# Edge sums of attention step 0: bitwise AND of the u8 blocks and a ones-column matmul instead of block products and a masked diagonal

## The chip, the cores and the metric

The kernel runs on one core of a Trainium2 chip. A core has five engines that run their own instruction queues: TensorE (PE in the profile, with its weight loads as PEld), VectorE (DVE), ScalarE (ACT), GpSimd (POOL) and SyncE (SP, which only issues DMAs here). The metric is the device time of the whole program in microseconds; lower is better.

## The reference, cut to what matters

A graph network of four layers on N = 4096 nodes with D = 256 features and a 0/1 adjacency matrix. Each layer's result is added to x and normalised.

```python
# layer 1: two steps of attention (A keeps the top of each row's softmax)
R = S + I;  R = R / R.sum(-1)              # S is the adjacency matrix here
for n in range(2):
    A  = top_p_attention(Xa, W1, W2, W3)
    Xf = R @ Xf
    Xa = A @ Xa
    Z  = Z + Xf @ U1[n].T + Xa @ U2[n].T
...
# layer 2
neighbor_node_features = adj @ node_features
neighbor_edge_features = einsum('ij,ji->i', adj, edge_features)   # edge_features is adj
support = concat(node_features, neighbor_node_features, neighbor_edge_features)
return support @ weight + bias
```

The change concerns the einsum: the edge sum of node i is the number of j with adj[i,j] and adj[j,i] both 1. It doesn't depend on features, and layer 2 reads it from the tile `nef` (128 partitions x 32 row tiles).

## The kernel before

Rows come in 32 tiles of 128. Columns come in 8 chunks of 512, called g0 to g7 here; a chunk has GP = 4 blocks of 128x128. Layer 0 runs to about 378 us, step 0 of layer 1 from there to about 1340 us, then step 1, then layers 2 and 3.

Step 0 is one software pipeline over the row tiles (`run_step`, with `pieces` for one tile's turn). In one turn TensorE goes through the chunks; in each chunk it computes logits for the tile two ahead (L381), adds gathered rows of x weighted by attention for the tile whose top entries are known (L730, weights from VectorE's dg, L728), and does the R product of the tile whose turn it is (`neighbours`). Between these, pieces for other tiles are hung into chosen chunks (`ops`): the exponentials (ScalarE L419), the choice of the top 16 entries (VectorE MAX8 L400, and two FIND_INDEX8 at L497 over rows of 4096), the flag of rows that need more entries (TensorE L559 and L560, VectorE L562 to L567) whose numbers GpSimd scatters into a list in DRAM (`list_d`, L573, 128 rows of 4 bytes), the 16 gathers of 128 rows of 1 KB (GpSimd L639, eight buffers: gather k+8 is emitted behind product k), and afterwards the mixing with U (TensorE L791, VectorE h at L793) and the keys of the new rows (TensorE L799). The first four row tiles of step 0 have only their R product, while the pipeline fills.

`neighbours(n, i, g, acc_r, pn, xf)` does one chunk of the R product for row tile i. Every second chunk SP loads a u8 tile adj8 (L648, three buffers). ScalarE casts 512 columns to float32r (`a`, L650), and four matmuls of 128x512 add into acc_r (L653), with xf held as a high and a low half of 256 columns each. L655 adds the identity's share at the end.

In step 0 it also computes the edge sums. Every fourth chunk GpSimd loads 256 KB of the transposed blocks as u8 (adjn8, L659, two buffers); ScalarE casts 512 columns (`b`, L662); four matmuls of 128x128 multiply blocks of `a` by blocks of `b` and add into the bank pn (`nef_ps`, L665). The edge sums are the diagonal of the sum.

`r_end` ends the tile: ScalarE scales one half of acc_r into xf_new (L674), VectorE adds the other (L675), VectorE multiplies pn by the identity and sums its rows into a column of nef (L679), SP stores xf_new (L681). acc_r and nef_ps each have one PSUM bank in step 0, so the next tile's first product waits until L675 has read acc_r. The same functions serve step 1, without pn.

Step 1 begins by loading the keys from DRAM (k_d), transposing them into kS (L1059), and loading xa (L1066).

Every engine takes its own queue in order, but that order isn't the order of the text: instructions of different pieces are interleaved on each engine when the program is built.

Of the kernel before, what the change touches and what calls it, by code (L numbers as in the profile page):

```python
# [11 lines left out]
F32 = mybir.dt.float32  # L12
I32 = mybir.dt.int32
U8 = mybir.dt.uint8
F32R = mybir.dt.float32r
AF = mybir.ActivationFunctionType
ALU = mybir.AluOpType
AX = mybir.AxisListType
# [3 lines left out]
P = 128  # L22
# [26 lines left out]
def gnn_stack(ctx, tc, x, adjt, adjn, w0, b0, w1, w2t, w3t, u1t, u2t, ln_g, ln_b, w2, b2, w3, b3, out):  # L49
# [3 lines left out]
    nc = tc.nc  # L53
    N = x.shape[0]
    NT = N // P
    LC = min(512, N)
    NLC = N // LC
# [9 lines left out]
    dram = ctx.enter_context(tc.tile_pool(name="dram", bufs=1, space=DRAM))  # L67
    ps_two = ctx.enter_context(tc.tile_pool(name="ps_two", bufs=1, space=PSUM))
    ps_acc = ctx.enter_context(tc.tile_pool(name="ps_acc", bufs=1, space=PSUM))
    ps_tr = ctx.enter_context(tc.tile_pool(name="ps_tr", bufs=2, space=PSUM))  # L70
# [7 lines left out]
    def half(bank):  # L78
        turns[bank] ^= 1
        return (mm_bank if bank == "mm" else acc_bank)[:, turns[bank], :]  # L80
# [10 lines left out]
    ident = const.tile([P, P], F32, name="ident")  # L91
    make_identity(nc, ident)
    ones_col = const.tile([P, 1], F32, name="ones_col")
# [5 lines left out]
    nef = const.tile([P, NT], F32, name="nef")  # L99
# [12 lines left out]
    list_d = [dram.tile([N + P, 1], I32, name=f"list{n}_d") for n in range(STEPS)]  # L112

    adj8_d = [dram.tile([P, NT, P], U8, name=f"adj8_{it}_d") for it in range(NT)]
    h_d = dram.tile([N + P, D], F32, name="h_d")
    k_d = dram.tile([N + P, P], F32, name="k_d")

# [5 lines left out]
    def rows(t, it):  # L123
        return t[it * P : (it + 1) * P, :]

    def all_rows(t):
        return t.rearrange("(t p) d -> p t d", p=P)
# [86 lines left out]
    with tc.tile_pool(name="l0", bufs=1) as l0, tc.tile_pool(name="l0w", bufs=2) as l0w:  # L214
# [9 lines left out]
        for c in range(2):  # L224
            ps = half("mm")
# [10 lines left out]
        def l0_main(it):  # L236
            acc = ps_acc.tile([P, 512], F32, tag=("acc", "nef")[it % 2], name="acc")

            W = J0 * P
            sums = l0w.tile([P, W], F32, tag="sums", name="sums")  # L240

            now = {}

            def piece(it, c):

                if c % 2 == 0:
                    now["a8"] = a8 = l0w.tile([P, 2 * JP, P], U8, tag="a8", name="a8", bufs=5)
                    s = slice(c * JP, (c + 2) * JP)
                    nc.gpsimd.dma_start(a8, adjt[it, :, s, :])
                    nc.sync.dma_start(adj8_d[it][:, s, :], a8)  # L250
                a = l0w.tile([P, JP, P], F32R, tag="adjt", name="a", bufs=4)
                nc.scalar.copy(a, now["a8"][:, c % 2 * JP : (c % 2 + 1) * JP, :])  # L252
                return a

            def partial(c, a):
                a = a.bitcast(F32).rearrange("p j i -> p (j i)")
                for k in range(0, JP * P, W):
                    if c == 0 and k == W:
                        nc.vector.tensor_add(sums, a[:, :W], a[:, W : 2 * W])
                    elif c > 0:  # L260
                        nc.vector.tensor_add(sums, sums, a[:, k : k + W])
                if c + 1 == NJP:
                    for k in (W // 2, W // 4):
                        nc.vector.tensor_add(sums[:, :k], sums[:, :k], sums[:, k : 2 * k])

            adj_matmul(l0w, acc, it, lambda jt: x0h[:, jt, :], piece, partial)
            return acc, sums
# [40 lines left out]
        for it in range(NT + 1):  # L308
            if it >= 1:
                agg = l0_agg(acc, l0_degrees(it - 1, sums))  # L310
            if it < NT:
                acc, sums = l0_main(it)
# [9 lines left out]
    with tc.tile_pool(name="l1", bufs=1, reuse_waits="tile") as l1:  # L322

        cur = {"late": False, "n": 0, "nef_done": False}
# [9 lines left out]
                                channel_multiplier=-1)  # L334
        ident_r = l1.tile([P, P], F32R, name="ident_r")
        nc.vector.tensor_copy(ident_r, ident)
        upto = l1.tile([P, PAD], F32, name="upto")
        nc.gpsimd.iota(upto, pattern=[[1, PAD]], base=0, channel_multiplier=0, allow_small_or_imprecise_dtypes=True)

# [9 lines left out]
        def load_u(n):  # L349
            for name, src in (("u1", u1t), ("u2", u2t)):  # L350
                t = l1.tile([P, 2, D], F32, tag=name, name=name)
                nc.scalar.dma_start(t, src[n].rearrange("(c p) o -> p c o", p=P))
                cur[name] = t
# [49 lines left out]
        QW = N // NQ  # L403

        spare_row = l1.tile([P, 4 * QW], U8, name="spare_row")
# [236 lines left out]
        GP = LC // P  # L642

        def neighbours(n, i, g, acc_r, pn, xf):

            if g % 2 == 0:
                cur["a8"] = cur["w"].tile([P, 2 * GP, P], U8, tag="adj8", name="adj8", bufs=3)
                nc.sync.dma_start(cur["a8"], adj8_d[i][:, g * GP : (g + 2) * GP, :])  # L648
            a = cur["w"].tile([P, GP, P], F32R, tag="adjq", name="adjq", bufs=2)
            nc.scalar.copy(a, cur["a8"][:, g % 2 * GP : (g % 2 + 1) * GP, :])  # L650
            for j in range(GP):
                jt = g * GP + j
                nc.tensor.matmul(acc_r, a[:, j, :], xf[:, jt, :], start=(jt == 0), stop=False)  # L653
            if g + 1 == NLC:
                nc.tensor.matmul(acc_r, ident_r, xf[:, i, :], start=False, stop=True)  # L655
            if pn is not None:
                if g % (NLC // 2) == 0:
                    cur["b8"] = cur["w"].tile([P, NT // 2, P], U8, tag="adjn8", name="adjn8", bufs=2)
                    nc.gpsimd.dma_start(cur["b8"], adjn[i, :, g * GP : g * GP + NT // 2, :])  # L659
                b = cur["w"].tile([P, GP, P], F32R, tag="adjn", name="adjn", bufs=2)  # L660
                k = g % (NLC // 2) * GP
                nc.scalar.copy(b, cur["b8"][:, k : k + GP, :])  # L662
                for j in range(GP):
                    jt = g * GP + j
                    nc.tensor.matmul(pn[:, :P], a[:, j, :], b[:, j, :], start=(jt == 0),  # L665
                                     stop=(jt == NT - 1))

        def r_acc(i):

# [2 lines left out]
        def r_end(i, acc_r, pn):  # L672
            xf_new = work.tile([P, D], F32, tag="xf_new", name="xf_new", bufs=1)
            nc.scalar.activation(xf_new, acc_r[:, :D], AF.Copy, scale=rs[:, i : i + 1])  # L674
            nc.vector.scalar_tensor_tensor(xf_new, acc_r[:, D:], rs[:, i : i + 1], xf_new, op0=ALU.mult, op1=ALU.add)  # L675
            if pn is not None:

                junk = spare_row.bitcast(F32)[:, :P]
                nc.vector.scalar_tensor_tensor(junk, pn[:, :P], 1.0, ident, op0=ALU.mult, op1=ALU.mult,  # L679
                                               accum_out=nef[:, i : i + 1])  # L680
            nc.sync.dma_start(rows(xf_d, i), xf_new)  # L681

        def r_product(n, i, xf):
# [8 lines left out]
        def pieces(n, st, nxt, ops, rs_now=()):  # L692
# [60 lines left out]
            if with_r:  # L753
                r_end(i, acc_r, pn)
# [286 lines left out]
        for n in range(STEPS):  # L1041
            cur["n"] = n
            with tc.tile_pool(name=f"step{n}", bufs=2, reuse_waits="tile") as cur["w"], \
                    tc.tile_pool(name=f"late{n}", bufs=1, reuse_waits="tile") as cur["lw"]:
                es = [cur["w"].tile([P, N + PAD], F32, tag=f"e{k}", name="e", bufs=1) for k in range(2 + n)]
                if n == 0:
                    cur["xa"] = x1
                    cur["qs"] = [query(x1[:, i, :]) for i in range(2)]
                    cur["xf"] = load_halves(es[1], x1, None)
                else:  # L1050
                    cur["g"] = load_bcast(cur["lw"], ln_g, "g_sb")
                    cur["qs"] = first_queries(xa_d)
                    k_rows = es[1][:, :N].rearrange("p (t d) -> p t d", d=P)
                    for c in range(NLC):
                        s = slice(c * GP, (c + 1) * GP)
                        nc.sync.dma_start(k_rows[:, s, :], all_rows(k_d[:N, :])[:, s, :])
                        ps = ps_tr.tile([P, 4, P], F32, tag="tr", name="kt_ps")
                        for j in range(GP):
                            nc.tensor.transpose(ps[:, j, :], k_rows[:, c * GP + j, :], ident)  # L1059
                        k = kS[:, c * LC : (c + 1) * LC].rearrange("p (j d) -> p j d", d=P)  # L1060
                        (nc.vector.tensor_copy if c % 2 else nc.scalar.copy)(k, ps[:, :GP, :])
                    cur["xf"] = cur.pop("next")
                    cur["xa"] = xa = xpool.tile([P, NT, D], F32, tag="X", name="xa")
                    for c in range(NJP):
                        s = slice(c * JP, (c + 1) * JP)
                        nc.scalar.dma_start(xa[:, s, :], all_rows(xa_d[:N, :])[:, s, :])  # L1066
                load_u(n)
                run_step(n, es)

# [128 lines left out]
```

## Time and profile before

| what | us |
|---|---|
| median of 3 runs (lowest, highest) | 3308.88 (3306.8, 3313.18) |
| the profiled execution's time | 3340.46 |
| its span | 3338.8 |
| TensorE busy, whole span | 3024.1 |
| VectorE busy | 2395.2 |
| ScalarE busy | 1873.3 |
| L665, 1024 matmuls of 128x128 in step 0, busy | 150.0 |
| L679 in step 0, 32 instructions, busy | 9.0 |
| L662, 256 casts of 128x512, busy | 159.3 |
| L497, 64 searches in step 0, busy | 282.8 |

The profile is of one execution, which took 31.6 us longer than the median of the runs; sums of durations are to be held against its own span. The mean TensorE clock granted in it was 0.964 of full speed. Busy times of TensorE's matmuls overlap one another, since matmuls are pipelined and their ends are modelled; the distance between starts is what a matmul costs.

Costliest groups of step 0 on its edge sums, in the view that keeps shapes apart (columns: line, engine, operation, output and inputs, shapes, count, then busy us and mean ns of one, then the idle time before them and what ended it):

```profile
L662 ACT CAST adjn<-adjn 128x512 fp32r<-128x512 uint8 x256 | 159.3, 622 | 1.0 <-DMA adjn<-in_adjn 1.0
L665 PEld LDWEIGHTS nef_ps<-adjn,adjq 128*128 128x128 f32 x1024 | 157.3, 192 | 23.8 <-ACT adjn L662 0.6 <-issue 0.2
L665 PE MATMUL nef_ps<-adjn,adjq 128*128 128x128 f32 x1024 | 150.0, 266 | 0.0
L659 POOL DMA_DIRECT2D adjn<-in_adjn x64 | 37.6, 588 | 64.3 <-ACT adjn L662 50.0 <-ACT te L512 7.0 <-issue 6.9
```

### The profile page before, as it was taken

The page shows a single profiled execution, that of the slowest core. Times are in us where ns is not written, and L with a number is a line of the kernel's source. Part 1 is how long each engine was busy: PE and PEld are TensorE (multiplying, and loading weights), DVE is VectorE, ACT ScalarE, POOL GpSimd, SP SyncE. Part 2 cuts the span into 40 slices and gives each one's busy share as a digit, 9 for nine tenths or more (in the row PEclk, how much of TensorE's full clock was granted, in tenths as well). Part 3 has the DMA queues.
Part 4 walks back from the last instruction along what each step waited for, and adds up shares of the span by engine and source line. Part 5 has one row for each costly group of instructions (what it writes and reads, how often), then busy time and mean ns, then how long its engine had stood idle before and what let it go on. Part 6 is the DMA issues. An engine that isn't in the chain of part 4 may idle for free. (4 is left out here: it accounts for less than half of the span.)

```text
span 3338.8 us, 46384 instructions
## 1 busy us (share of the span) xinstructions
PE 3024.1 (91%) x14600; PEld 2462.3 (74%) x14600; DVE 2395.2 (72%) x7120; ACT 1873.3 (56%) x3162; POOL 781.6 (23%) x915
## 2 busy tenths in 40 slices
PE   6999888999999998779998898999999796999998
PEld 5888667777877777557887777877788554888886
DVE  7888858777777777346997888799799683444444
ACT  3555666766766665436555454555465333666664
POOL 1111245656666666100000001000100001000000
PEclk9999999999999998889999999999999898999999
DMA  9888366777777676331000211011111143333332
GB/s 174 139 142 138 71 103 119 134 125 135 135 133 123 122 134 144 94 116 42 25 23 21 32 29 37 28 31 37 29 34 34 32 142 117 114 109 106 100 110 81
DMA packets 247858, 300.17 MB, mean 90 GB/s; under 512 B 34672, under 2 KB 201520, under 8 KB 247600
## 3 DMA queue, kind: packets, MB, share of 16 engines
q0 software_dynamic: 46576, 104.94, 23.1%
q1 hardware_dynamic: 188800, 180.93, 18.7%
q10 hardware_dynamic: 12224, 11.23, 1.1%
q8 instruction: 118, 1.93, 0.3%
q14 instruction: 140, 1.15, 0.2%
HBM read 331.17 MB, written 66.45 MB: 119 GB/s over the span
## 5 line engine op out<-in xcount | busy, mean ns | idle before, releaser
L653 PE MATMUL acc_r<-xh,adjq 128*128 128x512 f32 x2048 | 616.2, 431 | 27.3 <-ACT adjq L650 20.4
L738 PE MATMUL acc_bank<-xa,at 128*128 128x256 f32 x2304 | 569.5, 388 | 29.5 <-ACT at L716 29.0
L639 POOL DMA_INDIRECT G<-x_d,cols x512 | 498.8, 974 | 334.1 <-PE acc_bank L730 155.8
L167 PE MATMUL acc<-xh,a 128*128 128x512 f32 x2048 | 516.5, 405 | 23.1 <-DMA a<-adj_d 15.6
L738 PEld LDWEIGHTS acc_bank<-xa,at 128*128 128x128 f32 x2304 | 424.9, 194 | 91.3 <-ACT at L716 39.9
L650 ACT CAST adjq<-adj 128x512 fp32r<-128x512 uint8 x512 | 315.8, 619 | 307.6 <-PE acc_r L653 95.5
L400 DVE MAX8 cand<-e 128x8 f32<-128x256 f32 x1024 | 381.8, 416 | 138.5 <-ACT e L382 115.2
L653 PEld LDWEIGHTS acc_r<-xh,adjq 128*128 128x128 f32 x2048 | 381.0, 192 | 126.9 <-ACT adjq L650 45.8
L167 PEld LDWEIGHTS acc<-xh,a 128*128 128x128 f32 x2048 | 384.8, 191 | 108.8 <-ACT xh L143 22.7
L382 ACT COPY e<-lg 128x512 f32<-128x512 f32 x552 | 320.2, 586 | 204.4 <-PE lg L381 173.4
L191 POOL TENSOR_TENSOR rstd<-ve,mhalf 128x1 f32<-128x1 f32 x168 | 103.3, 615 | 1377.5 <-DVE ve L189 1332.9
L381 PE MATMUL lg<-kS,q 128*128 128x512 f32 x1104 | 396.1, 444 | 21.0 <-ACT e L382 11.6
L1078 ACT CAST a<-a 128x1024 fp32r<-128x1024 uint8 x256 | 267.8, 1048 | 158.0 <-PE acc L167 121.3
L730 PE MATMUL acc_bank<-G,dg 128*128 128x256 f32 x1024 | 277.1, 392 | 32.8 <-DVE dg L728 13.8
L497 DVE FIND_INDEX8 cols<-top,e 128x8 uint32<-128x4096 f32 x64 | 282.8, 4419 | 0.0
L730 PEld LDWEIGHTS acc_bank<-G,dg 128*128 128x128 f32 x1024 | 194.0, 193 | 82.5 <-DMA G<-x_d,cols 20.3
L167 PE MATMUL acc<-yh,a 128*128 128x512 f32 x1024 | 233.7, 390 | 0.0
L716 ACT COPY at<-at_ps 128x512 f32<-128x512 f32 x296 | 173.8, 589 | 102.5 <-PE at_ps L713 100.8
L252 ACT CAST a<-a 128x1024 fp32r<-128x1024 uint8 x128 | 133.6, 1049 | 156.4 <-PE acc L167 121.4
L167 PEld LDWEIGHTS acc<-yh,a 128*128 128x128 f32 x1024 | 192.1, 188 | 39.7
L381 PEld LDWEIGHTS lg<-kS,q 128*128 128x128 f32 x1104 | 184.5, 194 | 45.2 <-ACT e L382 20.6
L713 PE MATMUL at_ps<-ident,e 128*128 128x128 f32 x1184 | 183.5, 279 | 14.7 <-DVE e L630 14.6
(281 smaller groups left out, 4634.2 us busy)
## 6 DMA issues: line engine op xcount, KB each, us to landing
adj<-adj_d SPq DMA_DIRECT2D x256, 128.0 KB
a<-adj_d SPq DMA_DIRECT2D x256, 128.0 KB
a<-in_adjt POOLq DMA_DIRECT2D x64, 256.0 KB
adj_d<-a SPq DMA_DIRECT2D x64, 256.0 KB
adjn<-in_adjn POOLq DMA_DIRECT2D x64, 256.0 KB
x_d<-x SPq DMA_DIRECT2D x64, 128.0 KB
G<-x_d,cols POOLq DMA_INDIRECT x512
xf_d<-xf_new SPq DMA_DIRECT2D x64, 128.0 KB
```

Of the source, the lines that this page charges most:

```text
L167: nc.tensor.matmul(acc, a[:, j, :], halves(jt), start=(jt == 0), stop=(jt == NT - 1))
L381: nc.tensor.matmul(pl[:, :LC], q[k], kS[:, s], start=(k == 0), stop=(k == 1))
L382: nc.scalar.copy(l[:, s], pl[:, :LC])
L400: nc.vector.max(dst[:, 8 * g : 8 * g + 8], src[:, g * GW : (g + 1) * GW])
L497: nc.vector.max_index(st["at"][:, 8 * r : 8 * r + 8], t8, st["e"][:, :N])
L639: nc.gpsimd.indirect_dma_start(out=g, out_offset=None, in_=x1_d, in_offset=bass.IndirectOffsetOnAxis(ap=st["at"][:, k : k + 1], axis=0))
L650: nc.scalar.copy(a, cur["a8"][:, g % 2 * GP : (g % 2 + 1) * GP, :])
L653: nc.tensor.matmul(acc_r, a[:, j, :], xf[:, jt, :], start=(jt == 0), stop=False)
L713: nc.tensor.transpose(ps[:, j, :], e[:, (g * G + j) * P : (g * G + j + 1) * P], ident)
L730: nc.tensor.matmul(acc_a, dg[:, k % 4, :], st["G"][k], start=(k == 0), stop=(k == KEPT - 1))
L738: nc.tensor.matmul(acc_a, ats[g][:, j, :], cur["xa"][:, jt, :], start=(jt == 0), stop=(jt == NT - 1))
L1078: nc.scalar.copy(a, a8)
```

## The change

Both inputs of the edge sum are 0 or 1, so the product of two elements is their AND, and the sum over j can be taken by a column of ones.

- Every second chunk of step 0 VectorE computes the bitwise AND of the adj8 tile and the matching half of adjn8, in place in adjn8, as 128x256 words of 32 bits (128 instructions). The load of adjn8 is emitted ahead of it, and so ahead of the chunk's casts.
- ScalarE's cast of `b` is the same instruction on the ANDed bytes.
- TensorE's four 128x128 products a chunk become one matmul: a column of 128 ones, times `b`'s 512 columns, added over the chunks into one row of 512 in pn. Each column of the row holds a quarter of a node's sum.
- At the tile's end ScalarE copies the row out of PSUM, into the spare row, and SP stores it to a row of `nef_d` in DRAM. VectorE's masked sum is gone.
- At the start of step 1 SP loads the 32 rows of 512; VectorE adds the four parts of each; TensorE transposes 32x128; VectorE copies the result to nef.

The lines after the change: adjn8 load L656, AND L659, acc_r's matmuls L664, cast of `b` L670, ones matmul L671, xf_new L680, row copy L684, store L685; searches L500, h L798, keys L804.

```diff
+    nef_d = dram.tile([NT, LC], F32, name="nef_d")
...
+        ones_r = l1.tile([P, 1], F32R, name="ones_r")
+        nc.vector.tensor_copy(ones_r, ones_col)
...
             if g % 2 == 0:
                 cur["a8"] = cur["w"].tile([P, 2 * GP, P], U8, tag="adj8", name="adj8", bufs=3)
                 nc.sync.dma_start(cur["a8"], adj8_d[i][:, g * GP : (g + 2) * GP, :])
+                if pn is not None:
+
+                    if g % (NLC // 2) == 0:
+                        cur["b8"] = cur["w"].tile([P, NT // 2, P], U8, tag="adjn8", name="adjn8", bufs=2)
+                        nc.gpsimd.dma_start(cur["b8"], adjn[i, :, g * GP : g * GP + NT // 2, :])
+                    k = g % (NLC // 2) * GP
+                    a32, b32 = (t.rearrange("p j i -> p (j i)").bitcast(I32) for t in (cur["a8"], cur["b8"][:, k : k + 2 * GP, :]))
+                    nc.vector.tensor_tensor(b32, b32, a32, op=ALU.bitwise_and)
             a = cur["w"].tile([P, GP, P], F32R, tag="adjq", name="adjq", bufs=2)
...
             if pn is not None:
-                if g % (NLC // 2) == 0:
-                    cur["b8"] = cur["w"].tile([P, NT // 2, P], U8, tag="adjn8", name="adjn8", bufs=2)
-                    nc.gpsimd.dma_start(cur["b8"], adjn[i, :, g * GP : g * GP + NT // 2, :])
                 b = cur["w"].tile([P, GP, P], F32R, tag="adjn", name="adjn", bufs=2)
                 k = g % (NLC // 2) * GP
                 nc.scalar.copy(b, cur["b8"][:, k : k + GP, :])
-                for j in range(GP):
-                    jt = g * GP + j
-                    nc.tensor.matmul(pn[:, :P], a[:, j, :], b[:, j, :], start=(jt == 0),
-                                     stop=(jt == NT - 1))
+                nc.tensor.matmul(pn[:1, :LC], ones_r, b.rearrange("p j i -> p (j i)"), start=(g == 0), stop=(g + 1 == NLC))
...
             if pn is not None:
 
-                junk = spare_row.bitcast(F32)[:, :P]
-                nc.vector.scalar_tensor_tensor(junk, pn[:, :P], 1.0, ident, op0=ALU.mult, op1=ALU.mult,
-                                               accum_out=nef[:, i : i + 1])
+                row = spare_row.bitcast(F32)[:1, QW - LC :]
+                nc.scalar.copy(row, pn[:1, :LC])
+                nc.sync.dma_start(nef_d[i : i + 1, :], row)
             nc.sync.dma_start(rows(xf_d, i), xf_new)
...
+                    parts = es[2][:NT, :LC]
+                    nc.sync.dma_start(parts, nef_d)
+                    sums = es[2][:NT, LC : LC + P]
+                    nc.vector.tensor_reduce(sums, parts.rearrange("t (j i) -> t i j", i=P), axis=AX.X, op=ALU.add)
+                    ps = ps_tr.tile([P, 4, P], F32, tag="tr", name="nef_ps")
+                    nc.tensor.transpose(ps[:, 0, :NT], sums, ident[:NT, :NT])
+                    nc.vector.tensor_copy(nef, ps[:, 0, :NT])
```

## The prediction

> **What bounds the kernel now.** I read the busy row first, then the groups of instructions, then the windows of step 0 (which runs from about 378 to 1340 us), then the timeline of single tiles.
>
> ```profile
> PE 3024.1 (91%) x14600; PEld 2462.3 (74%) x14600; DVE 2395.2 (72%) x7120; ACT 1873.3 (56%) x3162; POOL 781.6 (23%) x915
> ```
>
> ```profile
> 560.00:660.00 100.00, 92.42 (x488) 77.98 (x486) 79.86 (x221) 71.18 (x142) 62.00 (x68) 1.00 0.75 138
> 800.00:900.00 100.00, 93.61 (x496) 79.26 (x495) 78.10 (x235) 67.68 (x136) 62.04 (x67) 1.00 0.76 140
> 1320.00:1400.00 80.00, 50.76 (x187) 36.73 (x186) 40.38 (x118) 31.53 (x50) 25.23 (x24) 0.79 0.42 115
> ```
>
> The windows' columns are length, then busy time of PE, PE's weight loads, VectorE, ScalarE and GpSimd, the granted TensorE clock, DMA share and GB/s. In step 0 TensorE is busy 92 to 94% of the time and VectorE 78 to 80%: TensorE bounds, with little slack behind it. The third window shows the clock at 0.79 where TensorE is idle a third of the time. Two starts of L679 that lie 25 tiles apart, 562.95 and 1280.30 us, give the pace: 28.69 us a tile.
>
> One tile on VectorE, and the queue of GpSimd around the next list scatter (start, length, engine, line, operation, then in brackets the idle time before it):
>
> ```profile
> 821.90 0.47 DVE L675 SCALAR_TENSOR_TENSOR xf_new<-acc_r,rs,xf_new 128x256 f32<-128x256 f32 x1
> 822.29 0.28 DVE L679 SCALAR_TENSOR_TENSOR spare_row<-nef_ps,ident 128x128 f32<-128x128 f32 x1
> ...
> 822.96 4.42 DVE L497 FIND_INDEX8 cols<-top,e 128x8 uint32<-128x4096 f32 x1
> ...
> 828.55 4.42 DVE L497 FIND_INDEX8 cols<-top,e 128x8 uint32<-128x4096 f32 x1
> 833.01 0.43 DVE L793 TENSOR_TENSOR h<-mm_bank,x 128x256 f32<-128x256 f32 x1
> ```
>
> ```profile
> 841.04 1.00 POOL L573 DMA_INDIRECT list_d<-ids,slots  x1 [0.53 <-issue]
> 842.35 0.96 POOL L639 DMA_INDIRECT G<-x_d,cols  x1 [0.30 <-PE acc_bank L730]
> ...
> 848.09 0.60 POOL L659 DMA_DIRECT2D adjn<-in_adjn  x1
> ```
>
> The reader should see two things. xf_new (L675) frees the only acc_r bank; after it come two searches of 4.42 us, then h, which releases TensorE's L799 at 833.49. And the 256 KB load of adjn's second half (g4 to g7; "h1" below) is issued 7 us after the scatter of the list, in the same software queue.
>
> **What the Trainium skill says.** "DMA: Bandwidth & Descriptors", section "Queues, rings and completion order": on each DMA engine descriptors are taken in ring order. So h1 queues behind the scatter's 128 rows and four gathers. The DMA view agrees in effect: from 841 to 852 us the software queue moves 209 packets, from 852 to 860 us 531. Its "Specifications" say that transfers under 512 B make the engine read, modify and write; the scatter's rows have 4 bytes, and the lull of some 11 us follows each of three scatters that I looked at (812.19, 841.04, 868.53; packets flow again at about 824, 852.5, 879). The cause isn't shown by the trace; the lull is. "TensorE: Matmul & The Clock Gate", the table that opens the page, row "Engine queue depth": ScalarE and VectorE take their queues strictly in order, so whatever stands behind a waiting AND waits too.
>
> **The change part by part.**
> TensorE: for each 512 columns (g) four matmuls at L665 become one of 512 columns. Weight-load starts in the timeline of a tile at full clock space an L665 group by 0.57 us; one 512-column matmul of the acc_r groups costs 0.21 to 0.23 us (0.91 us for four). Saved: 0.34 us a g, 2.7 us a tile, 87 us in 256 g. TensorE's own floor is about 25.9 us a tile (8 x 2.70 for acc_r, nef, lg and G, and 4.3 for the rest), 23.2 after. If nothing else took over, 28.69 would become about 26.2.
>
> VectorE: gains an AND of 128x256 words for each two g. Rows of that shape: L1107 421 ns, L295 426 ns, so 0.42 us, and 4 a tile make 1.7 us; the page "VectorE: DVE Perf Modes", section "The TRN2 errata", prices a 32-bit tensor_tensor by (N+151)/0.96 ns, 424 ns for 256, which agrees. L679 goes (0.36 us with its accumulator read). Busy 22 us a tile becomes 23.4. ScalarE keeps its casts and gains a copy of one row (512 elements, like the 0.58 us of L382): 19.5 to 20.1 us. GpSimd is unchanged: 18 issues, about 23.2 us a tile with 0.30 us gaps. SP gains a 2 KB store a tile, beside loads of 128 KB, behind no wait that the casts need: nothing.
>
> Step 1's start: one load of 32 rows (small loads here land after about 2.3 us), a reduction of 128x4 in about 0.7 us, a transpose 0.3, a copy 0.2, all while step 1 loads keys and xa. Between 0 and 4: I take +2. Layer 0, the rest of step 1, and layers 2 and 3 keep their order on every engine: 0.
>
> **Where the AND stands.** This decides. I compared the order of instructions on each engine. The AND of a pair of g is emitted when the pair's adj8 load is, ahead of the casts. For the row tiles 11 to 31 (21 tiles) VectorE's order is now: AND(g0), AND(g2), the last MAX8 pieces, AND(g4), **then xf_new of the tile before, then search 0**, AND(g6), search 1, h. For tiles 4 to 10 AND(g4) stands after the second search, where h1 has long landed. AND(g4) needs h1. Before, h1 was first needed by ScalarE's cast for g4, 16 to 19 us after the end of the tile before (L655); now it is needed about 1.5 us after it. When does h1 land? Counting the software queue's packets after the lull (gathers 2 to 5 of the tile, then h1's 128 packets of 2 KB) puts it at about 827.8, 856.9 and 883.7 us: 15.2 to 15.9 us after each list scatter, 7.6 to 8.7 us after L655. So AND(g4) waits some 6 to 7 us, and behind it wait xf_new (so TensorE's next acc_r, which stands ahead of all its other work), both searches, h, and L799.
>
> That is a loop, since h1 is issued behind the list, and the list behind the searches. Starting when AND(g4) can run: xf_new +0.4, search 0 from +1.2, search 1 from about +7 (the spacing before is 5.6, and an AND is between), h ends at +12.1, L799 at +12.2; then the flags' matmuls (L559, L560) after one more acc_r group and the rest of TensorE's pieces, +3.3; the slots and the scatter +1.4: the list goes out at about +16.9. (Before, the list left 7.5 us after L799, but there GpSimd was issuing gathers back to back until it; at a longer period it has room. If it doesn't, +19.) h1 lands 15.5 later: 14 if fewer gathers come between, 17 if all 16 engines are as busy as now. Sum 16.9 + 15.5 = 32.4 us, from 30.9 to 36 at the corners. TensorE would idle some 8 of 32 us a tile, in one piece; by the window at 1320 us that can cost clock, 0 to 1.5 us, which I put into the upper end only.
>
> Sum: 21 tiles x (32.6 - 28.7) = +82; 7 tiles with cover x -2 = -14 (half a us short of the 2.5 possible, since VectorE and ScalarE are near their own limits); the first four tiles, which carry only the R product and run at 12 to 16 us each, +2 (TensorE saves 2.7 but the ScalarE casts, 16 x 0.62 a tile, and the ANDs set their pace); step 1's start +2. Together +72 on the profiled execution's 3340.5 us (span 3338.8), which lies 31.6 us or 0.95% above the median of the runs shown, 3308.88. Scaled by 0.99: +71, so 3380 us.
>
> **The rivals.**
> A, faster: h1 lands in time or AND(g4)'s wait isn't felt, for instance because the lull after the scatter shrinks when TensorE's waits thin out the other DMAs, or the POOL queue runs ahead and issues h1 earlier than 7 us after the list. For it: POOL's idle times show it waits for TensorE at times (3.31 us for acc_bank at 835.6). Against: the order puts four gathers between list and h1, and the lull has been there after each list looked at. Then 28 tiles gain 2.2 to 2.7 us: -62 to -75, +4 for the two ends; about 3244 us. Chance 0.22.
> B, a milder wait: h1 lands 13 us after the list, period 30: 21 x 1.3 - 14 + 4 = +17, about 3325 us. Chance 0.17.
> C, slower still: TensorE's idle piece lowers the clock and the gathers, which also stand behind the list, come late (before, TensorE waited for them at 622.73 by 0.98 us): period 35 gives 21 x 6.3 - 10 = +122, about 3430 us. Chance 0.09. The point from which the loop decides at all is a landing 12 us after the list: below it the period is set by the engines.
> D, the gain and the wait cancel: 0.04.
> The loop as worked out, 3340 to 3415 us: 0.48.
>
> **How the numbers follow.** The likeliest case gives 3380; its own range, with the unknown landing (14 to 17) and list (16.9 to 19), is 3325 to 3435. Eight in ten needs part of A as well: 3255 to 3435 leaves out about half of A and half of C. A difference of 0.2% (6.6 us) is what can be told from none. Slower: B, C and the loop, 0.74; I take a little off B's lower edge, 0.73. Faster 0.23, same 0.04.
>
> **What would show it.** In the changed kernel's trace: VectorE idle before the AND (L659) with releaser DMA adjn, several us in each tile from the 12th on and near nothing before; acc_r's weight load (L664) waiting for VectorE's xf_new (L680); the row copies (L684) about 32 us apart in the late tiles and about 26.5 in tiles 4 to 10; the nef matmul near 0.22 us a g; busy PE in the windows of step 0 down to some 75%. If the late row copies are 26 to 27 us apart and the AND never waits, rival A is right and my landing time or my reading of the order is wrong. If the AND waits for adj8's load from SP rather than adjn, the place is right and the cause is another queue.

## The result, and the profile after

| | before | after | ratio, 95% interval |
|---|---|---|---|
| median us | 3307.84 | 3460.03 | 1.0461 [1.0447, 1.0474] |
| profiled execution's span | 3338.8 | 3460.0 | |
| its mean TensorE clock | 0.964 | 0.937 | |

The change makes the kernel 152 us slower; 3380 was forecast. The busy row of the page after the change:

```profile
PE 2999.4 (87%) x13833; PEld 2394.9 (69%) x13833; DVE 2422.3 (70%) x7187; ACT 1886.4 (55%) x3194; POOL 787.6 (23%) x915
```

The view of windows, two stretches in the middle of step 0 (columns as before: length, PE, weight loads, VectorE, ScalarE, GpSimd, granted clock, DMA share, GB/s):

```profile
800.00:900.00 100.00, 78.55 (x345) 62.09 (x345) 68.55 (x198) 58.66 (x118) 52.50 (x56) 0.87 0.63 113
1000.00:1100.00 100.00, 71.14 (x314) 56.16 (x314) 63.20 (x182) 55.66 (x112) 48.77 (x53) 0.83 0.59 105
```

Before, TensorE was busy 93.61% from 800 to 900 us. Every engine is less busy now, and so are the DMA engines: no engine of the core is full, they wait for one another. The groups of step 0 say for what (line, engine, operation, tiles, shapes, count, busy us and mean ns, then idle time before and its releasers):

```profile
L664 PE MATMUL acc_r<-xh,adjq 128*128 128x512 f32 x1064 | 376.0, 470 | 195.5 <-DVE xf_new L680 182.9 <-DVE xh L145 9.1 <-ACT xh L144 1.7
L671 PE MATMUL nef_ps<-adjn,ones_r 128*1 128x512 f32 x256 | 108.4, 424 | 3.5 <-ACT spare_row L684 3.4
L659 DVE TENSOR_TENSOR adjn<-adjn,adj 128x256 int32<-128x256 int32 x128 | 51.2, 417 | 206.3 <-DMA adjn<-in_adjn 204.3 <-DMA adj<-adj_d 1.9
```

The AND costs 417 ns as priced. But VectorE stood 204 us in front of ANDs until adjn's load had landed (21 of them in the first four tiles), and TensorE stood 183 us in front of acc_r's matmuls until VectorE had done xf_new. In step 0 before, acc_r's weight loads waited 4.6 us for xf_new in all:

```profile
L653 PEld LDWEIGHTS acc_r<-xh,adjq 128*128 128x128 f32 x1034 | 195.5, 193 | 50.8 <-DVE xf_new L675 4.6 <-ACT adjq L650 3.5 <-issue 3.0
```

One turn in VectorE's timeline after the change:

```profile
942.28 0.43 DVE L659 TENSOR_TENSOR adjn<-adjn,adj 128x256 int32<-128x256 int32 x1 [8.65 <-DMA adjn<-in_adjn]
942.63 0.48 DVE L680 SCALAR_TENSOR_TENSOR xf_new<-acc_r,rs,xf_new 128x256 f32<-128x256 f32 x1
...
943.09 4.42 DVE L500 FIND_INDEX8 cols<-top,e 128x8 uint32<-128x4096 f32 x1
...
948.87 4.42 DVE L500 FIND_INDEX8 cols<-top,e 128x8 uint32<-128x4096 f32 x1
953.21 0.41 DVE L798 TENSOR_TENSOR h<-mm_bank,x 128x256 f32<-128x256 f32 x1
```

TensorE's timeline around it, and GpSimd's behind it:

```profile
943.16 2.08 PE L664 MATMUL acc_r<-xh,adjq 128*128 128x512 f32 x4 [8.61 <-DVE xf_new L680]
...
947.03 1.28 PE L664 MATMUL acc_r<-xh,adjq 128*128 128x512 f32 x4
...
955.07 0.61 PE L804 MATMUL mm_bank<-w3t_sb,xt 128*128 128x128 f32 x4
...
958.46 0.28 PE L562 MATMUL mm_bank<-bad,ones_sq 128*128 128x1 f32 x2
```

```profile
960.16 1.00 POOL L576 DMA_INDIRECT list_d<-ids,slots  x1 [0.30 <-issue]
961.47 0.95 POOL L642 DMA_INDIRECT G<-x_d,cols  x1 [0.30 <-PE acc_r L664]
...
966.61 0.60 POOL L656 DMA_DIRECT2D adjn<-in_adjn  x1
```

The next AND(g4) runs at 975.09. This is the forecast's loop, step by step: AND 942.28, list 960.16 (+17.9), next AND 975.09 (+14.9). Over tiles 11 to 31 the list leaves 18.3 us after the AND (17.7 to 19.9) and the next AND runs 16.3 us after the list (14.9 to 17.6): 34.6 us a turn, where 28.57 were needed before.

### The profile page after: what moved, and what is told of

It is laid out like the page before. It is cut to its first block, busy times and chain, and to the rows that moved or that the text cites. A ratio compares the mean times of both kernels' runs of the same rounds, so it can differ in the third digit from the quotient of the medians.

```text
span 3460.0 us, 45142 instructions
## 1 busy us (share of the span) xinstructions
PE 2999.4 (87%) x13833; PEld 2394.9 (69%) x13833; DVE 2422.3 (70%) x7187; ACT 1886.4 (55%) x3194; POOL 787.6 (23%) x915
## 5 line engine op out<-in xcount | busy, mean ns | idle before, releaser
L664 PE MATMUL acc_r<-xh,adjq 128*128 128x512 f32 x2048 | 651.5, 446 | 213.2 <-DVE xf_new L680 182.9
L664 PEld LDWEIGHTS acc_r<-xh,adjq 128*128 128x128 f32 x2048 | 394.8, 200 | 324.9 <-DVE xf_new L680 192.1
L642 POOL DMA_INDIRECT G<-x_d,cols x512 | 506.4, 989 | 422.3 <-PE acc_bank L735 287.7
L168 PE MATMUL acc<-xh,a 128*128 128x512 f32 x2048 | 515.6, 405 | 23.9 <-DMA a<-adj_d 16.1
L735 PE MATMUL acc_bank<-G,dg 128*128 128x256 f32 x1024 | 288.6, 406 | 35.3 <-DMA G<-x_d,cols 21.1
L500 DVE FIND_INDEX8 cols<-top,e 128x8 uint32<-128x4096 f32 x64 | 282.8, 4418 | 0.0
L735 PEld LDWEIGHTS acc_bank<-G,dg 128*128 128x128 f32 x1024 | 207.0, 205 | 86.2 <-DMA G<-x_d,cols 27.5
L384 PEld LDWEIGHTS lg<-kS,q 128*128 128x128 f32 x1104 | 199.3, 198 | 62.1 <-ACT e L385 21.2
L718 PE MATMUL at_ps<-ident,e 128*128 128x128 f32 x1184 | 183.6, 279 | 17.4 <-DVE e L633 17.3
```

The source lines that it names most:

```text
L168: nc.tensor.matmul(acc, a[:, j, :], halves(jt), start=(jt == 0), stop=(jt == NT - 1))
L384: nc.tensor.matmul(pl[:, :LC], q[k], kS[:, s], start=(k == 0), stop=(k == 1))
L500: nc.vector.max_index(st["at"][:, 8 * r : 8 * r + 8], t8, st["e"][:, :N])
L642: nc.gpsimd.indirect_dma_start(out=g, out_offset=None, in_=x1_d, in_offset=bass.IndirectOffsetOnAxis(ap=st["at"][:, k : k + 1], axis=0))
L718: nc.tensor.transpose(ps[:, j, :], e[:, (g * G + j) * P : (g * G + j + 1) * P], ident)
L735: nc.tensor.matmul(acc_a, dg[:, k % 4, :], st["G"][k], start=(k == 0), stop=(k == KEPT - 1))
```

## The experiments

Ratios are to the kernel before in the same set of runs. Before took 3308 us in the first set and 3328 to 3341 in the three sets below, so times of different sets are compared only where the text says so. The last column is the mean spacing of xf_new from tile 10 to tile 30 in the profile.

| kernel | ratio, 95% interval | us per late tile |
|---|---|---|
| before (first profile; second profile) | 1 | 28.67; 28.42 |
| after | 1.0461 [1.0447, 1.0474] | 34.59 |
| after again, another set | 1.0399 [1.0380, 1.0418] | 34.68 |
| AND alone, block products kept | 1.0777 [1.0749, 1.0804] | 38.01 |
| AND written into adj8 | 0.9956 [0.9942, 0.9969] | 27.47 |
| adjn8 in quarter tiles | 1.0089 [1.0072, 1.0106] | 29.70 |
| no AND (column sums of adjn alone) | 0.9892 [0.9875, 0.9908] | 26.17 |
| after, spare slots spread | 1.0021 [1.0012, 1.0030] | 31.56 |
| before, spare slots spread | 0.9823 [0.9784, 0.9862] | 28.09 |
| AND in adj8, spread | 0.9761 [0.9736, 0.9786] | 27.51 |
| quarters, spread | 0.9632 [0.9607, 0.9656] | 26.31 |
| no AND, spread | 0.9608 [0.9583, 0.9634] | 26.25 |
| quarters, AND in adj8, spread | 0.9606 [0.9581, 0.9631] | 26.49 |

### Before, profiled again

No edit.

> The kernel before, unchanged, profiled a second time. The forecast scaled a sum made on the profiled execution of before (3340.5 us) by 0.99 to the median (3308.9); the profiled execution of the changed kernel took 3460, the same as its own median. Theory odd draw: the first profile was a slow draw, and this one lies within 10 us of 3308, with a tile period in step 0 near 27.6 us in place of 28.6. Theory profiling: taking a profile slows a step that TensorE bounds; this one is again 20 us or more above 3308, with a period of 28.5 or more.

The profiled execution took 3335.1 us and the median of before in this set is 3330.3; the late tiles take 28.42 us. The numbers are close to those of the second theory, but its reason falls: here the runs without a profile are just as long. The first profile, at 3340.5 us, fits this set and the later ones. So the 31.6 us between it and the first runs look like a difference between sets of runs, and not something to take off a sum. Why the first runs were faster isn't shown.

### The AND in adj8: the same work in another order

```diff
-                    nc.vector.tensor_tensor(b32, b32, a32, op=ALU.bitwise_and)
...
-                nc.scalar.copy(b, cur["b8"][:, k : k + GP, :])
...
+                if g % 2 == 1:
...
+                    nc.vector.tensor_tensor(a32, a32, b32, op=ALU.bitwise_and)
+                    for h in (g - 1, g):
+                        b = cur["w"].tile([P, GP, P], F32R, tag="adjn", name="adjn", bufs=2)
+                        nc.scalar.copy(b, cur["a8"][:, h % 2 * GP : (h % 2 + 1) * GP, :])
+                        nc.tensor.matmul(pn[:1, :LC], ones_r, b.rearrange("p j i -> p (j i)"), start=(h == 0), stop=(h + 1 == NLC))
```

The AND stands in the odd chunks now, behind both casts of adj8.

> The same ANDs, loads and ones matmuls, but the AND is written into adj8 in place of adjn8, after both casts of adj8. Its order on VectorE then comes out otherwise: AND(g4) stands after both searches and h of the same turn, and only AND(g0) is ahead of xf_new. Loop theory (AND(g4)'s wait for h1 ahead of xf_new closes a loop through the list): the wait before xf_new is gone, the late tiles take 26 to 27.5 us each, and the time is 3215 to 3265 us. Rival price of the work (the ANDs, the row copies and the ones matmuls are what costs): nothing of that is removed, so it stays above 3400.

Ratio 0.9956: the loss of 4 to 5% is gone with no instruction less. Written over adj8, the AND must wait for ScalarE's casts of that tile, and these for buffers that acc_r's products free, so AND(g4) can't be put ahead of the previous tile's xf_new. Waits of VectorE for adjn's load: 0.4 us in all. The price of the work as the cause falls. The time is above the range expected, 3315 us where 3215 to 3265 stood: step 0's waits of TensorE show what is late next (us in all, times, longest; from 380 to 1500 us; 12.8 us before):

```profile
PE acc_bank L736 <- DMA G<-x_d,cols: 59.0, 38, 7.3
```

These are gathers that stand behind the list, and now behind h1 too, which is issued one gather behind it. Tiles 4 to 10 also take 31.0 us each (28.7 before).

### Quarter tiles: the load ahead of the list

```diff
-                    if g % (NLC // 2) == 0:
-                        cur["b8"] = cur["w"].tile([P, NT // 2, P], U8, tag="adjn8", name="adjn8", bufs=2)
-                        nc.gpsimd.dma_start(cur["b8"], adjn[i, :, g * GP : g * GP + NT // 2, :])
+                    cur["b8"] = cur["w"].tile([P, 2 * GP, P], U8, tag="adjn8", name="adjn8", bufs=5)
+                    nc.gpsimd.dma_start(cur["b8"], adjn[i, :, g * GP : (g + 2) * GP, :])
```

> adjn8 in five quarter tiles of 128 KB in place of two halves of 256 KB, so that the quarter with g4 and g5 is issued ahead of the list scatter in GpSimd's order; AND(g4) still stands ahead of xf_new and of the second search on VectorE. Loop theory: what matters is that h1 queued behind the scatter; with the quarter ahead of it the AND finds its data, the waits fall from 8.6 us a tile to under 2, the period to 26 to 28 us, and the time is 3220 to 3290. Rival slow load (the load takes over 10 us wherever it is issued, since it casts): the AND still waits 5 us or more a tile, and the time stays above 3380.

Ratio 1.0089, between the two. No AND waits for adjn any more; 27 of them wait for another load, 118 us in all. The timeline of one (SPq is a DMA issue of SP):

```profile
900.89 1.02 POOL L576 DMA_INDIRECT list_d<-ids,slots  x1 [0.30 <-issue]
...
902.26 0.32 SPq L651 DMA_DIRECT2D adj<-adj_d  x1
...
909.32 0.42 DVE L658 TENSOR_TENSOR adjn<-adjn,adj 128x256 int32<-128x256 int32 x1 [5.02 <-DMA adj<-adj_d]
```

The 128 KB of adj8, on SP's own queue, issued 1.4 us behind the scatter, took 7.1 us to land. In the 16 late turns in which it was issued at that distance it took 6.5 to 9.2 us. So the lull isn't only a matter of ring order in GpSimd's queue, as the forecast had it: it holds back the other queue too.

### No AND

```diff
-                    nc.vector.tensor_tensor(b32, b32, a32, op=ALU.bitwise_and)
```

> The change without its ANDs: column sums of adjn alone, so the edge sums are plain column counts here. Everything else of the change stays. Loop theory: no instruction ahead of xf_new waits for h1; period 26 us, time 3215 to 3255, and the loads land as late after the list as before (15 us). Rival price of the work: the four ANDs of a tile are 1.7 us of VectorE, which is not the bound, so taking them out leaves the time above 3400.

Late tiles at 26.17 us, as expected and as the forecast's rival A had them; the whole at 0.9892, 3293 us, above the 3215 to 3255. The first eleven tiles took as long as before (xf_new of tile 10 at 707.4 us, 706.6 before). The saving on TensorE is real, and it needs no more than that nothing waits.

### The spare slots spread

A scatter writes 128 row numbers. Rows that need no more entries go to spare slots behind the list, one for each partition and 4 bytes apart.

```diff
-    list_d = [dram.tile([N + P, 1], I32, name=f"list{n}_d") for n in range(STEPS)]
+    list_d = [dram.tile([N + P * P, 1], I32, name=f"list{n}_d") for n in range(STEPS)]
...
-        nc.gpsimd.iota(spare, pattern=[[0, 1]], base=N, channel_multiplier=1, allow_small_or_imprecise_dtypes=True)
+        nc.gpsimd.iota(spare, pattern=[[0, 1]], base=N, channel_multiplier=P, allow_small_or_imprecise_dtypes=True)
```

> The changed kernel; only the spare slots of the list (where rows that need no more entries are put, nearly all of a scatter's 128) are 512 B apart in DRAM in place of 4 B. Instructions and their order on each engine are the same. Loop theory with crowded slots (the lull after a scatter is 128 writes of 4 bytes into one 512 B stretch): the lull shrinks, h1 lands 8 to 12 us after the list in place of 16.3, AND(g4) waits under 2 us a tile in place of 8.6, the period falls from 34.6 to 26 to 28 us, and the time is 0.97 to 0.99 of before. Rival small writes (each 4-byte write is slow wherever it goes): landing and waits stay, the time stays 1.04 to 1.05 of before. Rival price of the work: also 1.04 or more.

Ratio 1.0021 in place of 1.04 to 1.046, with the same instructions in the same order on each engine; 0.97 to 0.99 was expected. So the same writes of 4 bytes cost less when they don't all go into one short stretch. But less than half of this gain is the loop's. Of the 130 us between the two profiles of the changed kernel (3460.0 and 3329.8), 60 lie in step 0 and 70 behind it, 64 of these in step 1, which scatters into a list of its own. VectorE's waits (who, for what, us in all, times, longest) in the changed kernel, and below it in the changed kernel with spread slots:

```profile
DVE adjn L659 <- DMA adjn<-in_adjn: 204.3, 28, 11.1
```

```profile
DVE adjn L659 <- DMA adjn<-in_adjn: 111.0, 25, 8.5
```

The AND now runs 13.0 us after the list, not 16.3, and the late tiles take 31.6 us: 3 us better, and 3.6 us above the range expected. Of the 13 us, 6.6 are the four gathers that GpSimd issues between list and h1, and 6.4 the load itself. The loop is still closed.

> The kernel before with the same spread slots. Loop theory: before had only the gathers waiting on the lull (TensorE waited for them by about 10 us in the whole of step 0) and the period's spread above 27.5; the time is 0.985 to 1.0 of before. If it were below 0.975, the gain of the next runs would be the spread's own and not the change's. Rival small writes: no change, 0.998 to 1.002.

Ratio 0.9823, just under the 0.985 to 1.0 expected, with an interval that reaches into it. So 1.8% was to be had in the kernel before, without the change. Little of it lies in step 0: of the 80 us between the two profiles (3338.8 and 3258.4) step 0 has 18, and step 1, from its first xf_new to its last, 56 (1211 to 1156 us). There ScalarE had waited for adj8 (us in all, times, longest; 1390 to 2595 us), and no longer does:

```profile
ACT adjq L650 <- DMA adj<-adj_d: 25.4, 7, 5.9
```

A version of the change must be held against 0.982, too. The changed kernel with spread slots is then still 2.0% or 72 us slower (3333.7 and 3261.5 us in this set), and 21 late tiles at 31.6 in place of 28.1 us make 73.

> The AND written into adj8 and the slots spread. With the AND in adj8 TensorE waited for gathers behind the list (55 us). Loop theory with crowded slots: these waits fall to under 20 us, the late tiles go from 27.4 to 26 to 26.8 us, and the time is 0.97 to 0.985 of before. Rival small writes: 0.995 as without the spread.

Ratio 0.9761, within the expectation by time. TensorE's wait for gathers fell from 59.0 to 3.8 us. But of the 72 us between the profiles with and without spread slots only 17 lie in step 0, and the late tiles stay at 27.5 us: in them TensorE now waits 57.8 us for ScalarE's copy xt ahead of the mixing (L797). Where the gathers were late, the copy is late now.

### The AND alone

```diff
-                nc.tensor.matmul(pn[:1, :LC], ones_r, b.rearrange("p j i -> p (j i)"), start=(g == 0), stop=(g + 1 == NLC))
+                for j in range(GP):
+                    jt = g * GP + j
+                    nc.tensor.matmul(pn[:, :P], a[:, j, :], b[:, j, :], start=(jt == 0),
+                                     stop=(jt == NT - 1))
```

The masked diagonal of `r_end` is as before, and there is no row copy and no sum at the start of step 1.

> The AND alone: the ANDs as in the change, but the four block products, the diagonal and no row copy as before (the product of a block with the ANDed block gives the same diagonal). VectorE's order again has AND(g4) ahead of xf_new. Loop theory: the AND's wait alone closes the loop; the period is 33 to 37 us and the time 1.035 to 1.07 of before, so that the ones matmul had no part in the loss. Rival price of the work (the loss comes from the ones matmul, the row copy or its PSUM wait): the ANDs alone cost at most their 1.7 us of VectorE, hidden; 0.998 to 1.01.

Ratio 1.0777, above even the range for the loop; late tiles 38.0 us. In one turn the list leaves 23.1 us after the AND (919.45 to 942.59), where it took 17.9 with the ones matmul: pieces that the order puts between AND and xf_new add 1.7 us, TensorE's way from its first acc_r group to the flags takes 17.6 us in place of 15.3, and the scatter comes 3.0 us after the flags in place of 1.7. So the ANDs at this place make the loss by themselves, and the shorter edge sums on TensorE took part of it back, since its pieces up to the flags lie in the loop.

### The change again, and the versions that gain

> The changed kernel itself, once more, since kernels before have taken 3308 us in the first runs and 3330 in later ones. Loop theory: the loop of 34.6 us (list 18.3 us after the AND, landing 16.3 after the list) is there again and the ratio to before is 1.04 to 1.047. Theory same pace: the loop is made of transfers and searches, which keep their pace where TensorE-bound stretches run slower, so that the time is 3455 to 3470 again and the ratio 1.037 to 1.042. Theory scaled: everything is slower alike, 3480 to 3490 and 1.045 to 1.048.

3471.7 us against 3340.9: 131 us more, 1.0399. The loop is the same to 0.1 us (34.68), and list to AND is 16.1. Before took 33 us more in this set than in the first, after only 12 us more. The time lies 1.7 us above the range of the theory of the same pace and below the other's. But the loop's 21 turns fill 725 of the 3460 us, so a pace of its own could keep back some 7 of the 33 us (an estimate by its share). Why before differs more between the sets than the changed kernel stays open.

> The change without its ANDs (column sums of adjn alone) and with the spare slots spread: what the saving on TensorE is worth when nothing waits for h1 or for the list. Loop theory: 28 tiles save up to 2.5 us against the spread kernel before, 0.9823 of before, so 0.958 to 0.972 of before and late tiles at 25.5 to 26.3 us. Rival (VectorE, ScalarE or the order of pieces bound as soon as TensorE is shorter): 0.975 or more.

Ratio 0.9608, late tiles 26.25 us: what TensorE's saving is worth with no AND and a shorter lull. Before with spread slots was run in another set; against it this is 1.6% by the times (3210.0 and 3261.5 us) and 2.2% by the two ratios.

> AND in adj8, adjn8 in four quarter tiles, slots spread. The load for g4 and g5 is issued ahead of the list, those for g6 and g7 one gather behind it. If the remaining loss of the AND in adj8 with spread slots (0.976) is late loads and gathers, the time is 0.965 to 0.974 of before; if it is the order on ScalarE and VectorE, it stays at 0.974 to 0.978.

Ratio 0.9606, better than expected, and the fastest that computes everything: 3207.6 us, 1.7% under before with spread slots by the times and 2.2% by the ratios. It reaches the version that leaves the AND out. A window of step 0:

```profile
900.00:1000.00 100.00, 95.06 (x443) 73.80 (x441) 87.19 (x262) 77.23 (x153) 75.24 (x83) 0.98 0.71 144
```

TensorE is back at 95%, and VectorE at 87% isn't far behind.

> The change with adjn8 in five quarter tiles and the slots spread; AND(g4) still ahead of xf_new. With quarters alone the AND waited for adj8's load (118 us in all), issued 1.4 us behind the list on SP's queue and landing 7 us later. Loop theory with crowded slots on all queues: adj8 lands in 2 to 4 us, the wait falls below 40 us in all, and the time is 0.97 to 0.985 of before. Rival (adj8 waits for its own issue, not for the lull): 1.0 or more.

Ratio 0.9632, better than expected, with the AND still ahead of xf_new: its waits for adj8 fell from 118 to 31.6 us. The same three lines as above, from a turn in which adj8's load was again issued 1.4 us behind the scatter:

```profile
999.11 1.02 POOL L576 DMA_INDIRECT list_d<-ids,slots  x1 [0.30 <-issue]
...
1000.48 0.32 SPq L651 DMA_DIRECT2D adj<-adj_d  x1
...
1003.80 0.45 DVE L658 TENSOR_TENSOR adjn<-adjn,adj 128x256 int32<-128x256 int32 x1 [1.29 <-DMA adj<-adj_d]
```

It lands within 3.3 us where it took 7.1. In the nine late turns in which an AND waited for a load issued 1.1 to 1.5 us behind the scatter, this took 3.0 to 4.1 us.

## Why the prediction was wrong

Its direction was right, and its mechanism in the main; its size was less than half of what came (71 of 152 us), and the time lay 25 us above the range.

- **TensorE's saving** (2.7 us a tile, floor near 26.2): right. With nothing waiting, late tiles take 26.2 to 26.5 us. (28.69 less 2.7 is 26.0; the 26.2 goes with the 2.5 that the sum used.) **The AND's price** (0.42 us): right, 0.417. The formula that the forecast took from the Trainium skill ("VectorE: DVE Perf Modes", "The TRN2 errata") is stated there for an add of 32-bit floats; it held for this AND.
- **Where the AND stands, and that it closes a loop through the list**: right. The waits are where it put them, taking the AND out or moving it takes the loss away, and the AND alone makes it.
- **The loop's length**, the step that failed first, "16.9 + 15.5 = 32.4 us", was mis-sized. Measured 18.3 + 16.3 = 34.6. The first term had the searches as the path, and they were not late: h ended 11.6 us after the AND (mean of the 21 late turns), where +12.1 was laid out, and L804 didn't wait for it. TensorE's own queue was the path. From xf_new on it worked without a gap and came to L804 at +13.3 (laid out +12.2), to the flags at +16.7 (+15.5), and the list left at +18.3 (+16.9). It starts each turn slowly: after 8.6 us of idling the first acc_r group took 2.08 us, a later one 1.28. The view of windows shows two stretches of equal length at the start of the turn above. In the first the granted clock is 0.50 and acc_r's matmuls start 0.43 us apart, in the second 1.00 and 0.23:

```profile
943.16:946.39 3.23, 3.23 (x8) 2.35 (x9) 3.23 (x1) 0.00 (x0) 0.00 (x0) 0.50 0.12 41
946.39:949.62 3.23, 3.23 (x18) 2.64 (x17) 3.23 (x8) 3.07 (x5) 2.10 (x2) 1.00 0.14 41
```

The slow stretch lasts 2.8 to 5.6 us in the late turns, 4.2 on average. With 2.8 us of it the flags come at +16.0, with 5.6 at +17.3, so about half of it is lost: 2.1 us a turn by this estimate, more than the 1.4 us that the first term lacked. The forecast had put this, as 0 to 1.5 us, into the upper end alone. Of the second term, h1's issue was as laid out (6.6 us behind the list); it landed 9.7 us later, 0.8 us over in all, and why isn't shown. So the line "21 tiles x (32.6 - 28.7) = +82" (written with 32.6; its own 32.4 makes +78) became 21 x (34.53 - 28.57) = +125, from the row copies of after and L679 of before.

- **The first eleven tiles**, "+2" for four of them and "7 tiles with cover x -2 = -14" for the rest: their sum of -12 came out, by luck. By the ends of the R product the first four cost +13, and the next seven gained 25. The ANDs of the first four tiles already waited 21 us for adjn, for which the forecast had no term. In the repeat, against before profiled again, it was +13 and -19. Behind the last tile of step 0 it was +8 (+2 forecast): the reduction (1.0 us) and the transpose stand beside the keys' last casts, and 5 of the 8 us lie ahead of these, where the two profiles of before differ by as much. The four terms make 125 + 13 - 25 + 8 = 121, the difference of the two spans (3460.0 - 3338.8).
- **"Scaled by 0.99"** is the other step that failed. It took 31.6 us off the changed kernel's time (3340.5 + 72 = 3412, made 3380), as if a faster run shortened everything alike. The 3412 is 48 us under the 3460 that the changed kernel took with a profile and without: the loop's 43 and the end's 6, but for rounding. Before differed by 1% between sets (3307.8 to 3340.9), the changed kernel by 0.3% (3460.0 to 3471.7), so the difference is 121 us between the two spans, 131 in the last set and 152 in the first. What made before faster in the first set stays open.
- **What the Trainium skill says of ring order** ("DMA: Bandwidth & Descriptors", "Queues, rings and completion order", there of the queues that SP and ScalarE issue to) fits that h1 comes behind the list and the gathers. It doesn't explain the lull, which the forecast read with it: the lull held back SP's queue as well (7.1 us for adj8), and it shrank when the same 4-byte writes were spread (3.3 us), so the size of a write, from the page's "Specifications", doesn't explain it alone either.
- **Rival A** gave the late tiles rightly for the kernels without the loop. The kernel with no AND gained 38 us by the medians (3330.3 to 3292.7) and 53 by the two profiles of its set, where 65 were laid out; its first eleven tiles gained 4 to 8 us where 15 to 19 had been counted. What it gained further with spread slots lies mostly behind step 0 (61 of 70 us between its two profiles).

## What to carry to other kernels

An instruction that waits for a transfer costs what stands behind it in its engine's queue; so the order in the built queue, and not the line where it is written, tells whether a cheap operation is safe. Giving it an operand that is late by nature (here adj8 behind its casts) held it in its place with the same work (0.9956 in place of 1.04). An engine that idles in one piece each turn should be priced at the clock that it gets when it resumes. Where a scatter sends its idle rows to spare slots, try slots that lie far apart (512 B here). And a forecast made on one profile shouldn't be scaled to times of another set of runs.

## What the hardware showed that was not expected

A scatter of 128 writes of 4 bytes, those of spare rows within 512 B, slowed loads in both DMA queues: adj8's 128 KB took 7.1 us behind it, and 3.3 us with 512 B between the slots. From 2 to 10 us after the scatter was issued, the DMA queues moved 42 GB/s in the kernel before (mean of 19 late turns), where they had moved 175 in the 4 us ahead of it; with spread slots it was 95. The DMA engines weren't idle in the lull: from 843 to 851 us in before their share is 0.83, at 55 GB/s. What makes a short stretch of addresses slow isn't shown. Nothing but these addresses makes 1.8% of the kernel before (0.9823 [0.9784, 0.9862]) and 4% of the changed one (1.04 to 1.0021), about half or more of it in step 1 and not where the change is.
